# A graph network's fourth layer: the sums over edges one quad further behind their products

## The chip, the cores and the metric

The kernel runs on one core of a Trainium2 chip. The core has five engines that work side by side and wait for one another through semaphores: TensorE (PE in the profile; its weight loads are PEld), VectorE (DVE), ScalarE (ACT), GpSimd (POOL) and SyncE (SP). The metric is the device time of one execution in microseconds (us), the median of several runs.

## The reference

Four graph layers run one after the other on 8192 nodes and 262144 edges, which are sorted by their destination. Each layer adds a message sum to the node features (32 per node) and normalises. The change concerns the last one, layer 3, cut here to what it computes:

```python
h = relu(edge_feat @ W1 + b1)                      # E x 64
w = (h @ W2 + b2).reshape(e, 4, 8, 8)              # E x 256: four 8x8 matrices an edge
w_000, w_011, w_101, w_110 = w[:, 0], w[:, 1], w[:, 2], w[:, 3]
s_e, v_e = s[src], v[src]                          # gathered node features: 8 scalars, 8 vectors of 3
m0 = ALPHA * (einsum('ei,eio->eo', s_e * sh0, w_000) + C110 * einsum('eim,em,eio->eo', v_e, sh1, w_110))
m1 = ALPHA * (einsum('ei,em,eio->eom', s_e, sh1, w_011) + einsum('eim,eio->eom', v_e * sh0, w_101))
out0 = segment_sum(m0, dst) + SI_SCALE * (s @ si_w0)
out1 = segment_sum(m1, dst) + SI_SCALE * einsum('nim,io->nom', v, si_w1)
x = layernorm(x + concatenate([out0, out1]))
```

## The kernel before

Layers 0 to 2 come first and are done at about 4640 us of the profile. Layer 3 is the code from L748 (`cut = Carve()`) to the end of `raw_layers`. All its buffers are cut by hand out of one arena of SBUF, so the profile calls all of them `f_arena`; all PSUM is `bank`, eight banks of 512 words.

The edges stand in tiles of 128 (one edge a partition). Four tiles make a *quad* (512 edges), two quads a *group* (1024 edges), and eight quads a block of 32 tiles. There are NQ = 512 quads. One loop runs over the turns q; in each turn instructions are issued to all engines, and each engine carries out its own in that order. Waits are written out by hand: `mark` gives an instruction's number on its engine's semaphore, `after` waits for such numbers, and an engine skips a wait that it has already had.

What a turn q issues:

- **TensorE, hidden products** (`hidden`, L875, matmuls at L882), in even turns, for quads q+2 and q+3. ScalarE takes them from bank 2 through a ReLU into the buffers `hs` (L890).
- **TensorE, W2 products of quad q** (L906): four matmuls of 65 x 128 by 65 x 256, into one of two pairs of banks that take turns (`w_bank`). They wait for `hs` and for `w_free`, the end of VectorE's turn q-2, which read the same pair of banks.
- **GpSimd, gathers for quad q+12** (`fetch_rows`, L383): four indirect DMAs of 128 node rows each, released by the W2 products of quad q.
- **TensorE, sums over edges of quad c = q-3** (L915): four matmuls of a one-hot matrix `oh` (128 edges by 128 destinations) with the products `p` (128 edges by 344 columns), added up in bank 0 or 1 over the two quads of a group. They wait for VectorE's turn c+2 (`quad[c + 2]["v"]`), because the last 24 columns of `p` of quad c are written two turns after its other columns.
- **VectorE, a turn**: every eighth turn, the preparation of the next block (`factors`, L824 to L835), which waits for that block's gathers; the last 24 columns of `p` of quad q-2 (L930); a reduction for quad q-1 (L935); then, after the W2 products of q, five multiplications from PSUM into `p` and `pr` (L943, L946, three of L950) and the one-hot matrix of q (L505). The end of L505 is the mark `v` of the turn. Ahead of writing, a turn waits for the sums that last used its buffers, `quad[q - NP]["a"]`.
- **VectorE, a group's sums**: in every second turn, after its mark `v`, it reduces the bank of the group that ends with quad q-3 into `win` (L972, L973, L975), and sets the bank free (`agg_free`). Eight times in the layer the shifted windows are then summed on TensorE (`windows`, L495) and 1024 nodes are normalised (`normalize`, L454 to L464).

The buffers `p` and `oh` each have five copies (NP, NO). What the change touches is the number of those copies, the distance of 3 between W2 products and sums, and the turn in which VectorE takes up a group.

Of the kernel before, what the change touches and what calls it, by code (L numbers as in the profile page):

```python
# [105 lines left out]
def in_order(ctx: ExitStack, tc, x, a, w0, w1, b1, w2, si, keep):  # L106
# [34 lines left out]
    with tc.tile_critical():  # L141
        raw_layers(tc, x, a, w0, w1, b1, w2, si, m, bad)
# [3 lines left out]
def raw_layers(tc, x, a, w0, w1, b1, w2, si, m, bad):  # L146
# [438 lines left out]
    NO = 4  # L585
# [16 lines left out]
    def fetch_rows(g, h, let):  # L602

        if g < GG:
            G.after(let)
            gathers(ytab, row, g * GT // WT, g * GT % WT + h * GT // 2, GT // 2)
            if h == 1:
                landed[g] = under_way[-1]
# [30 lines left out]
    for g in range(GG + 2):  # L639
# [8 lines left out]
        h, bk, c = g % NO, (g // per) % 2, g % per  # L648
# [69 lines left out]
    for n, (l, c) in enumerate(seq):  # L718
# [8 lines left out]
        for s in range(64):  # L727
            if l == 1:
                q = s % 4
# [35 lines left out]
    a1 = cut(WT, 8)  # L765
    vm = cut(2, WT, 3, 8)
    MW = 344
    NP, NO = 5, 5
    p = cut(NP, 4, MW)
    pr = cut(2, 4, 64)  # L770
    red = cut(2, 4, 8)
# [22 lines left out]
    NQ = TT // 4  # L794
# [80 lines left out]
    def hidden(q):  # L875

        s = q // 8
        k = s % 3
        PE.after(batch[s]["e"], quad.get(q - 1, {}).get("h", h_free))
        for h in range(2):  # L880
            r = q % 4 + h
            ins = PE.e.matmul(bank[64 * h:64 * h + 64, 2, :], w1_s[r * D:(r + 1) * D, :],  # L882
                              ef[r * D:(r + 1) * D, k, (q % 8) // 4, :], start=True, stop=True,
                              tile_position=(r * D, 64 * h))
        pm = PE.mark(ins)
        if q % 8 == 6:
            ef_free[k] = pm
        for h in range(2):
            A.after(pm, quad.get(q + h - 4, {}).get("w"))
            quad[q + h] = dict(h=A.mark(A.e.activation(hs[0:64, (q + h) % 4], bank[64 * h:64 * h + 64, 2, :], AF.Relu,  # L890
                                                       bias=b1_s[64 * h:64 * h + 64])))
# [3 lines left out]
    factors(0)  # L895
    PE.after(c_in)
    hidden(0)
    for q in range(NQ + 4):

        if q % 2 == 0 and q + 2 < NQ:  # L900
            hidden(q + 2)
        if q < NQ:
# [4 lines left out]
            quad[q]["w"] = PE.mark(ins)  # L907
            quad[q]["k"] = k, wp
            fetch_rows(q + AHEAD)
        c = q - 3  # L910
        if 0 <= c < NQ:
            g = c // 2
            PE.after(quad[c + 2]["v"], agg_free[g % 2] if c % 2 == 0 else None)
# [14 lines left out]
        if 0 <= q - 2 < NQ:  # L928
            c = q - 2
# [35 lines left out]
                if s + 3 < NS:  # L965
                    fetch(s + 3)

        c = q - 3
        if 0 <= c < NQ and c % 2 == 1:
            g = c // 2  # L970
            V.after(quad[c]["a"])
# [483 lines left out]
```

## Time and profile before

| | |
|---|---|
| median of 3 runs | 7594.48 us (7588.88 to 7602.49) |
| the profiled execution | 7684.33 us, span 7682.3 us |
| PE busy | 5356.7 us (70% of the span) |
| DVE busy | 4365.5 us (57%) |
| POOL busy | 3983.9 us (52%) |
| ACT busy | 1629.8 us (21%) |
| layer 3: first W2 product, last sum over edges | 4637.5 us, 7660.9 us |
| layer 3: first and last gather issued | 4564.2 us, 7599.5 us |

All times inside the execution are microseconds from the start of the span. A row of the groups by line names line, engine, operation, what it writes and reads, shapes and count; then the busy time and the mean of one in ns; then the idle time of the engine just before these instructions, with who ended it. Each matmul of this layer is in fp32 and shows as two records, so the four of a quad are "x8". The recorded ends of matmuls are modelled. A row of the waits has the waiting engine and line, whom it waited for, the time in total, the number of waits and the longest. Shares of PEclk are tenths of TensorE's full clock, as granted in each fortieth of the span.

### The profile page before, as it was taken

To read this page: it belongs to the slowest core of one execution; us is meant where nothing else is said; L and a number is where in the kernel's file an instruction comes from. 1 tells how busy PE (TensorE), PEld (TensorE's weight loads), DVE (VectorE), ACT (ScalarE), POOL (GpSimd) and SP (SyncE) were. 2 spreads that over 40 slices of the span, in tenths; PEclk is the share of its full clock that TensorE was granted. 3 is DMA by queue.
4 is the path that set the end of the run, shared out by engine and by line. 5 is a ranking of instruction groups with operands and counts; after the bars stand their busy time and mean duration, and the time that the engine had idled before them with its cause. 6 is when DMAs were issued, how large, how long until landed. Compare 5 with 4: busy or idle time off the path is not lost.

```text
span 7682.3 us, 85779 instructions
## 1 busy us (share of the span) xinstructions
PE 5356.7 (70%) x34036; PEld 3776.5 (49%) x34036; DVE 4365.5 (57%) x8312; ACT 1629.8 (21%) x2812; POOL 3983.9 (52%) x4174
## 2 busy tenths in 40 slices
PE   5326565666666665665445768888888888888888
PEld 2115555555555555554222435555555555555555
DVE  3336666666666766765000005667666666666666
ACT  3213333333333333332000001111111111111111
POOL 3466565656565566651000016666666666666663
PEclk6556666666666667667777878999998999898999
DMA  8415554555455454557999961111111111111111
GB/s 279 149 41 145 135 148 138 145 138 148 138 143 149 135 149 134 148 137 268 433 431 429 401 265 20 24 24 24 23 24 24 24 24 24 24 24 23 24 24 19
DMA packets 290731, 999.29 MB, mean 130 GB/s; under 512 B 99021, under 2 KB 175886, under 8 KB 250638
## 3 DMA queue, kind: packets, MB, share of 16 engines
q1 hardware_dynamic: 155742, 916.89, 30.6%
q0 software_dynamic: 134144, 73.67, 10.4%
q8 instruction: 269, 4.41, 0.2%
q10 hardware_dynamic: 432, 3.15, 0.1%
q14 instruction: 144, 1.18, 0.1%
HBM read 521.39 MB, written 471.99 MB: 129 GB/s over the span
## 4 chain that ended last, share of the span: by engine, by line
PE 53%; DVE 12%; another core or an unknown queue 11%; DMA 10%; issue 8%; ACT 6%; POOL 0%; SPq 0%; DVEq 0%; ACTq 0%; POOLq 0%
PE bank L571 18%; PE bank L915 17%; PE bank L906 9%; DMA f_arena<-famat 6%; PE bank L882 3%; ACT f_arena L576 3%; DMA f_arena<-fcmat 3%; DVE f_arena L950 2%; ACT f_arena L575 2%; PE bank L730 2%; DVE f_arena L505 2%; PE bank L733 2%; DVE f_arena L946 1%; PE bank L657 1%
## 5 line engine op out<-in xcount | busy, mean ns | idle before, releaser
L383 POOL DMA_INDIRECT f_arena<-fxtab,f_src x2048 | 1959.1, 957 | 2146.6 <-DVE f_arena L786 1069.3
L383 POOL DMA_INDIRECT f_arena<-fytab,f_row x2048 | 1957.6, 956 | 1344.5 <-issue 548.4
L571 PE MATMUL bank<-f_arena 64*128 64x128 f32 x16384 | 1623.1, 374 | 959.3 <-issue 550.8
L571 PEld LDWEIGHTS bank<-f_arena 64*128 64x128 f32 x16384 | 1507.0, 279 | 1076.1 <-issue 899.3
L915 PE MATMUL bank<-f_arena 128*128 128x344 f32 x4096 | 1477.2, 508 | 320.3 <-DVE f_arena L505 307.2
L915 PEld LDWEIGHTS bank<-f_arena 128*128 128x128 f32 x4096 | 847.4, 211 | 790.4 <-DVE f_arena L505 364.0
L575 ACT ACTIVATE f_arena<-bank 128x512 bf16<-128x512 f32 x1024 | 613.0, 599 | 1973.2 <-PE bank L571 949.7
L906 PE MATMUL bank<-f_arena 65*128 65x256 f32 x4096 | 1011.3, 390 | 0.0
L906 PEld LDWEIGHTS bank<-f_arena 65*128 65x128 f32 x4096 | 769.5, 193 | 359.8 <-issue 226.7
L890 ACT ACTIVATE f_arena<-bank,f_arena 64x512 f32<-64x512 f32 x512 | 351.1, 686 | 2566.1 <-PE bank L882 955.0
L557 DVE TENSOR_TENSOR f_arena<-bank,f_arena 128x1024 f32<-128x1024 f32 x256 | 313.2, 1223 | 808.2 <-PE bank L571 323.9
L505 DVE TENSOR_TENSOR f_arena<-bank,f_rel 128x512 f32<-128x512 f32 (+1 forms) x768 | 659.0, 858 | 140.3 <-ACT f_arena L537 128.1
L576 ACT ACTIVATE f_arena<-bank 128x512 f32<-128x512 f32 x1024 | 611.5, 597 | 0.0
L559 DVE TENSOR_TENSOR f_arena<-bank,f_arena 128x2048 f32<-128x2048 f32 x256 | 586.6, 2291 | 8.8
L943 DVE TENSOR_TENSOR f_arena<-bank,f_arena 128x256 f32<-128x256 f32 x512 | 215.5, 421 | 651.0 <-PE bank L906 352.4
L950 DVE TENSOR_TENSOR f_arena<-bank,f_arena 128x256 f32<-128x256 f32 x1536 | 550.7, 414 | 0.0
L730 PE MATMUL bank<-f_arena,f_x_b 128*32 128x256 f32 x4096 | 295.0, 459 | 334.4 <-DMA f_arena<-famat 334.4
L657 PE MATMUL bank<-f_arena 128*128 128x96 bf16 x2048 | 252.0, 253 | 320.7 <-issue 173.8
L730 PEld LDWEIGHTS bank<-f_arena,f_x_b 128*32 128x32 f32 x4096 | 145.9, 132 | 472.5 <-DMA f_arena<-famat 309.5
L946 DVE TENSOR_TENSOR f_arena<-bank,f_arena 128x512 f32<-128x512 f32 x512 | 348.7, 681 | 0.0
L454 DVE TENSOR_TENSOR f_lnf<-bank,f_x_b 128x256 f32<-128x256 f32 x8 | 3.4, 424 | 606.4 <-PE bank L710 606.4
L657 PEld LDWEIGHTS bank<-f_arena 128*128 128x128 bf16 x2048 | 144.1, 118 | 413.3 <-issue 277.0
(133 smaller groups left out, 3539.5 us busy)
## 6 DMA issues: line engine op xcount, KB each, us to landing
famat<-f_arena SPq DMA_DIRECT2D x256, 1024.0 KB
fcmat<-f_arena SPq DMA_DIRECT2D x256, 512.0 KB
fytab<-f_arena SPq DMA_DIRECT2D x64, 1024.0 KB
f_arena<-fytab,f_row POOLq DMA_INDIRECT x2048
f_arena<-fxtab,f_src POOLq DMA_INDIRECT x2048
f_arena<-laid_ea SPq DMA_DIRECT2D x64, 512.0 KB
f_arena<-laid_ea SPq DMA_DIRECT2D x64, 64.0 KB
f_arena<-laid_xT ACTq DMA_DIRECT2D x1, 1024.0 KB, 8.3
```

Of the source, the lines that this page charges most:

```text
L383: return G.e.indirect_dma_start(out=dest, out_offset=None, in_=table, in_offset=bass.IndirectOffsetOnAxis(ap=ix, axis=0))
L505: return V.e.tensor_tensor(o, iota[:, None, :].to_broadcast([P, n, P]), rel[:, t:t + n, None].to_broadcast([P, n, P]), op=OP.is_equal)
L559: V.e.tensor_tensor(oh_l[:, b], iota[:, None, :].to_broadcast([P, 16, P]), meta_l[:, pp, k0:k0 + 16, None].to_broadcast([P, 16, P]), op=OP ...
L571: ins = PE.e.matmul(bank[:, bk + h, :].rearrange("p (c s j) -> p c s j", s=64, j=4)[:, :, :, j], oh_l[hs_, b, 4 * q + j, :], oh_k[hs_, b, ...
L575: A.e.activation(st_c[:, b, q], bank[:, bk:bk + 2, 0:256], AF.Copy)
L576: bank_free[units[0] % 2] = am = A.mark(A.e.activation(st_a[:, b, q], bank[:, bk:bk + 2, 256:512], AF.Copy))
L657: ins = PE.e.matmul(bank[:, bk, 3 * c * D:3 * (c + 1) * D], oh[:, h, t, :], xp[:, g % 4, t].rearrange("p c f -> p (c f)"), start=(t == 0), ...
L730: ins = PE.e.matmul(bank[q * D:(q + 1) * D, b, 0:256].rearrange("p (u h j) -> p u h j", h=2, j=4), x_b[:, s, :], mv[:, s], start=(s < 4), ...
L906: ins = PE.e.matmul(wp[:, t, :], hs[0:65, q % 4, t * P:(t + 1) * P], w2_s[0:65], start=True, stop=True)
L915: ins = PE.e.matmul(bank[:, g % 2, 0:MW], oh[:, c % NO, t, :], p[:, c % NP, t, :], start=(c % 2 == 0 and t == 0), stop=(c % 2 == 1 and t = ...
L946: V.e.tensor_tensor(pq[:, :, 0:128].rearrange("p t (o k) -> p t o k", k=16), wp[:, :, 0:128].rearrange("p t (o k) -> p t o k", k=16), a0[: ...
L950: V.e.tensor_tensor(pq[:, :, 128 + 64 * mm:192 + 64 * mm].rearrange("p t (o i) -> p t o i", i=8), wp[:, :, 192:256].rearrange("p t (o i) - ...
```

## The change

The sums over edges of quad c are issued in turn c+4 instead of c+3, behind the W2 products of quad c+4. VectorE takes up a group's sums in turn c+5, c being the group's last quad, instead of c+3; TensorE has issued that quad's sums one turn earlier, where before it issued them in the same turn. `p` and `oh` get a sixth copy each, and the loop runs for 518 turns instead of 516. What the sums wait for is written as before (`quad[c + 2]["v"]`), which is now VectorE's turn q-2 instead of q-1.

```diff
-    NP, NO = 5, 5
+    NP, NO = 6, 6
+    LAG3 = 4
...
-    for q in range(NQ + 4):
+    for q in range(NQ + LAG3 + 2):
...
-        c = q - 3
+        c = q - LAG3
         if 0 <= c < NQ:
             g = c // 2
             PE.after(quad[c + 2]["v"], agg_free[g % 2] if c % 2 == 0 else None)
...
-        c = q - 3
+        c = q - LAG3 - 1
         if 0 <= c < NQ and c % 2 == 1:
             g = c // 2
             V.after(quad[c]["a"])
```

## The prediction

> **What bounds the kernel now.** I first read the page's forty slices, to place layer 3.
>
> ```profile
> PE   5326565666666665665445768888888888888888
> DVE  3336666666666766765000005667666666666666
> POOL 3466565656565566651000016666666666666663
> PEclk6556666666666667667777878999998999898999
> ```
>
> From slice 25 on, PE is busy eight tenths, VectorE and GpSimd six: layer 3, from about 4640 us to the end. Nothing before it is changed. Next, the groups of instructions by line between 4640 and 7660 us, and TensorE's waits there.
>
> ```profile
> L383 POOL DMA_INDIRECT f_arena<-fxtab,f_src x2000 | 1913.8, 957 | 1062.9 <-issue 542.9 <-PE bank L906 268.4 <-PE bank L915 131.3
> L915 PE MATMUL bank<-f_arena 128*128 128x344 f32 x4093 | 1476.3, 508 | 320.3 <-DVE f_arena L505 307.2 <-issue 12.8
> L906 PE MATMUL bank<-f_arena 65*128 65x256 f32 x4092 | 1009.4, 389 | 0.0
> L943 DVE TENSOR_TENSOR f_arena<-bank,f_arena 128x256 f32<-128x256 f32 x512 | 215.5, 421 | 651.0 <-PE bank L906 352.4 <-PE bank L915 139.6 <-remote 83.3
> ...
> PE bank L915 <- DVE f_arena L505: 307.2, 138, 4.0
> ```
>
> TensorE waits almost only at L915 (sums over edges), for L505, the last VectorE instruction of a turn: 138 times, 307 us. VectorE waits 651 us for the W2 products, so the two wait for each other in a ring. GpSimd's waits other than its own issue end with TensorE. The last matmul of L915 starts at 7660.9 us and the first W2 product at 4637.5 us: 3023 us for 512 quads, 5.90 us each. The chain of waits between 6002 and 6020 us shows one stop of the ring.
>
> ```profile
> 6002.48 1.73 PE bank L906 x8
> 6004.21 2.32 PE bank L915 x8
> 6006.53 1.22 PE bank L882 x4
> ...
> 6009.79 0.61 DVE f_arena L505
> 6010.40 0.04 issue
> 6010.44 4.27 PE bank L915 x8
> ```
>
> Unhindered, a quad's W2 products take 1.73 us, its sums 2.32 us. After a stop the same eight records take 4.27 us, so a stop costs its idle time and 1.95 us more. Last, the timeline between 6018 and 6029 us (start, duration, idle before and who ended it):
>
> ```profile
> 6018.69 1.07 PE L882 MATMUL bank<-f_arena 32*64 32x512 f32 x4
> 6019.70 1.99 PE L906 MATMUL bank<-f_arena 65*128 65x256 f32 x8
> 6021.53 2.48 PE L915 MATMUL bank<-f_arena 128*128 128x344 f32 x8
> 6023.85 1.89 PE L906 MATMUL bank<-f_arena 65*128 65x256 f32 x8
> 6025.17 1.40 ACT L890 ACTIVATE f_arena<-bank,f_arena 64x512 f32<-64x512 f32 x2 [15.85 <-PE bank L915]
> 6025.26 0.42 DVE L943 TENSOR_TENSOR f_arena<-bank,f_arena 128x256 f32<-128x256 f32 x1 [5.54 <-PE bank L915]
> 6026.74 0.94 POOL L383 DMA_INDIRECT f_arena<-fxtab,f_src  x1 [0.30 <-issue]
> 6027.93 1.52 PE L915 MATMUL bank<-f_arena 128*128 128x344 f32 x2 [2.18 <-DVE f_arena L505]
> ```
>
> The hidden products (L882) end at 6019.76 by the record, but their reader on ScalarE starts at 6025.17. The W2 products end at 6021.69, and VectorE starts on them at 6025.26, 3.6 us later. TensorE's completions thus reach the others late at times, here by up to 5.4 us. The previous L882 (6006.53 to 6007.75 in the chain) was answered at 6007.93, within 0.2 us. The profile does not tell me why; I carry the lateness as an unknown.
>
> **What the Trainium skill says.** "TensorE: Matmul & The Clock Gate", What's actually happening: the array runs at half clock after about 3.4 us of little activity, and needs about as long of work to get back. The trace agrees in kind (4.27 against 2.32 us), but here a stop of 1 to 2 us is enough at times. "Perfetto Trace Analysis", Tensor Engine Instruction: a matmul's recorded end is estimated, and its semaphore comes when PSUM acknowledges the write. That allows the lateness; it doesn't give its 5.4 us. "DMA: Bandwidth & Descriptors", SWDGE vs HWDGE vs iDMA: GpSimd's cores write each descriptor of such a gather, so a gather occupies GpSimd. The trace agrees: 957 ns and 0.30 us to the next. "SBUF — State Buffer", SBUF: two separate sides: VectorE and GpSimd share a pair of ports, which one can hold against the other. The gathers' median is 945 ns against a minimum of 938, so hardly any of it shows here.
>
> **The change, part by part.**
>
> 1. The sums' wait. In turn q TensorE issues W2 of q, then the sums of q-3, which wait for VectorE's turn q-1. Afterwards they are the sums of q-4 and wait for turn q-2. W2 of q has already waited for that turn, since there are two W2 banks. So this wait is removed, and the first wait for turn q-1 is W2 of q+1, one set of sums later (2.32 us, with L882 3.3 to 3.5 us). In the stretch 6010.44 to 6027.93 us (three sets of sums, 17.49 us) the stop of 2.18 us is then covered by 2.32 us of sums, and the slow restart (1.95 us) goes: 13.4 us, 4.5 us a quad.
>
> 2. The new place of the wait. Ring: turn q-1 ends, W2 of q+1 (1.73), lateness L, VectorE's products L943 to L505 (6007.78 to 6010.40, 2.6 us): 4.4 us + L for two quads. TensorE's own two quads take 2 x (1.73 + 2.32) + 1.1 = 9.2 us. The ring is covered up to L = 4.8 us. At 5.4 us it costs 0.6 us, a short stop.
>
> 3. VectorE takes up a group's sums at q-5. TensorE did those in turn q-1, before W2 of q, whose completion VectorE has had. So the waits of L972 (about 240 us over the layer in all) go. They stand on VectorE, ahead of the next turn, and end with the ring; I don't count them twice. The bank is freed one turn later (L975): the sums of even q-4 need turn q-2's group sum, 0.8 us after that turn's end, behind the 1.73 us of W2. No wait while W2 takes longer than 0.8 us; without that cover, 0.8 us in every second turn (205 us).
>
> 4. Six buffers of p and oh for five: a buffer is reused in turn q after the sums of q-6, done in TensorE's turn q-2, as were those of q-5 before. No instruction is added; the cost is memory (1888 words a partition).
>
> 5. One more set of sums (2.3 us) behind the last products: +2.5 us once. The eight places where normalisation enters the ring stay. The gathers are still issued by GpSimd after W2 of q for quad q+12, the edge loads still by SyncE: both now earlier, as the turns are shorter. Nothing passes anything in their queues.
>
> What is late next: TensorE's floor is 512 x 4.6 = 2355 us, plus about 100 us at the eight normalisations (an estimate: some 10 us of stop and 4 us of L495 each), so 2455. GpSimd issues a gather every 957 + 300 ns, in undisturbed rows 1.25 us, so 5.0 us a quad. It starts 12 quads ahead, has 2000 to go from 4641 us, and so ends at 4641 + 2500 = 7141 us instead of 7599.5: no more than 458 us can go. The two floors are close, and VectorE's preparation of each eight quads (about 4 us) needs the last gather of them. For late completions, short stops and restarts I leave 60 us, an estimate (0.6 us of every fifth quad). Gain 458 - 60 = 398 us, 5.1 us a quad.
>
> The profiled execution took 7684.3 us for a span of 7682.3; with 398 less it would take 7286. The median is 7594.5, or 0.988 of it. I scale the gain: 393, so **7200 us**.
>
> **Rivals.**
>
> *A, as above*: TensorE runs on, and GpSimd's gathers become the bound. For: rows of 2.32 and 1.73 us whenever nothing is waited for, and GpSimd at 1.25 us. 7200 us, own range 7130 to 7300. Chance 0.62.
>
> *B, late completions keep half of it.* With L near 6 us in most turns the ring is 10.4 us for two quads, and stops with restarts bring it to about 5.5 us a quad: 0.4 x 512 = 205 us gained, 7390 us (7300 to 7480). For: more work without a pause could mean later completions. Against: the chain also shows prompt ones. 0.21.
>
> *C, GpSimd is quicker than its profile* (the 0.30 us between gathers partly the profiler's): TensorE's floor, 2455 for 3023 us, leaves 7040 to 7110 us. 0.05.
>
> *D, it does nothing*: the wait moves to W2 whole, which needs stops longer than 2.3 to 3.5 us throughout. Their mean is 307 / 138 = 2.2 us. 7590 us, 0.03.
>
> *E, slower.* Completions become later still because TensorE no longer pauses. The ring exceeds today's 11.8 us for two quads from L = 7.4 us on; at 8.2 us it is 12.6, 6.3 us a quad, +205 us: 7800 us. For: after the stops shown, completions are prompt, and a pause may be what lets them catch up. Against: 5.4 us is the longest in the stretch shown, and it came after TensorE had run for 15 us. 0.09.
>
> **How the numbers follow.** A measurement of this kernel can tell about 0.2% (15 us) from no change. Faster: A, B and C, 0.88. Same: D, 0.03. Slower: E, 0.09. The range 7110 to 7440 leaves out E, D, most of C and the upper part of B, about 0.2.
>
> **What would show it.** Step 1: L915's idle time falls from 320 us to below 60 us, and its mean from 508 ns towards 460 ns. Step 2: TensorE's waits for L505 stand at L906. Step 3: L972 has no idle time left. The bound: GpSimd's idle time goes down to its own issue (about 0.30 us each), the last gather starts near 7150 to 7200 us, and VectorE waits for gathers at the preparation. Wrong if L906 takes over more than 150 us of waits, if ScalarE's answers to L882 come later than 6 us as a rule (B, E), or if a gather takes clearly more than 957 ns.

## The result and the profile after

The kernel after takes 7578.29 us (median of 9 runs, 7571.73 to 7589.08), the kernel before in the same set of runs 7602.49 us (9 runs, 7588.46 to 7607.30). The ratio is 0.9973, with a 95% interval of 0.9963 to 0.9984: 24 us faster by the medians, where 393 us were forecast. The profiled execution of after took 7583.78 us for a span of 7581.8.

I measure layer 3 in all kernels as the time from the start of the first W2 product to the end of the last sum over edges, divided by 512 quads. It was 5.906 us a quad before (4637.5 to 7661.3 us) and is 5.793 after (4595.0 to 7561.0 us), 58 us less. Layer 3 also starts 42 us earlier, though nothing ahead of it was changed. The profiled execution of before was also 90 us above its median. Two single executions therefore differ by more than the change, and the 58 us are not its worth; the 24 us of the medians are.

One fact is needed to read the numbers below: later sets of runs executed the same kernel before in 6476 to 6489 us instead of 7602 to 7639, so I call this set and that of e1 to e4 the *first sets*, those of e5 to e16 the *later sets*, and compare only inside a set. In the code after, lines behind the loop's start have moved by one: hidden products L883, ScalarE L891, W2 products L907, sums L916, VectorE's products L944, a group's sums L973.

The forty slices of the page, after:

```profile
PE   5326665556555665654544867889989988888998
...
PEclk7557677777777777777777877999998999899989
```

TensorE has gone from eight tenths to between eight and nine. Next, the groups by line between 4640 and 7660 us; the columns are those of the tables above.

```profile
L383 POOL DMA_INDIRECT f_arena<-fxtab,f_src x1970 | 1892.8, 961 | 967.4 <-issue 541.5 <-remote 177.4 <-PE bank L907 175.8
L916 PE MATMUL bank<-f_arena 128*128 128x344 f32 x4056 | 1406.7, 489 | 65.4 <-issue 63.7
L907 PE MATMUL bank<-f_arena 65*128 65x256 f32 x4020 | 1048.4, 403 | 176.2 <-issue 161.0 <-DVE f_arena L505 14.2
...
L944 DVE TENSOR_TENSOR f_arena<-bank,f_arena 128x256 f32<-128x256 f32 x504 | 211.3, 419 | 829.7 <-remote 320.1 <-PE bank L907 318.7 <-PE bank L916 129.0
L973 DVE TENSOR_REDUCE f_arena<-bank 128x8 f32<-128x128 f32 x255 | 71.3, 280 | 6.7 <-PE bank L916 6.7
```

The 307.2 us in which the sums waited for L505 are gone. Only 14.2 us of waits for L505 stand at the W2 products. But TensorE now has 161.0 us at L907 and 63.7 us at L916 that end with "issue": it waited for no semaphore that the profile shows. VectorE waits longer for TensorE than before (829.7 against 651.0 us), and GpSimd still waits for it as well. All of them wait for TensorE, and TensorE hardly waits for them: 14.2 us here, and 53.7 us at the eight normalisations (L495).

The timeline of after, from 6003 us on (start, duration, then the idle time before):

```profile
6002.83 1.07 PE L883 MATMUL bank<-f_arena 32*64 32x512 f32 x4
...
6003.84 1.99 PE L907 MATMUL bank<-f_arena 65*128 65x256 f32 x8
...
6008.94 1.56 PE L907 MATMUL bank<-f_arena 65*128 65x256 f32 x6 [0.79 <-issue]
...
6011.84 0.59 PE L907 MATMUL bank<-f_arena 65*128 65x256 f32 x1 [1.34 <-issue]
...
6013.24 0.59 PE L907 MATMUL bank<-f_arena 65*128 65x256 f32 x1 [0.81 <-issue]
...
6014.64 1.88 PE L916 MATMUL bank<-f_arena 128*128 128x344 f32 x3 [0.81 <-issue]
...
6014.74 1.40 ACT L891 ACTIVATE f_arena<-bank,f_arena 64x512 f32<-64x512 f32 x2 [19.00 <-PE bank L907]
6014.83 0.43 DVE L944 TENSOR_TENSOR f_arena<-bank,f_arena 128x256 f32<-128x256 f32 x1 [5.32 <-PE bank L907]
```

The hidden products end at 6003.90 by the record; ScalarE, which had been idle for 19 us, gets them at 6014.74, 10.8 us later. The W2 products recorded up to 6005.83 are answered at 6014.83. Just ahead of these answers TensorE's records crawl: one matmul at 6011.84, one at 6013.24. Over the layer, the time from a hidden product's recorded end to ScalarE's start has a median of 0.82 us, a third quartile of 5.0 and a maximum of 10.9; before they were 0.09, 2.5 and 7.2. So either only the news of TensorE's completions came late, or its recorded starts and ends ran ahead of what it had done, by up to 10.9 us and further than before. e1 decides between the two.

### The profile page after: what moved, and what is told of

The parts are those of the page before. It is cut to its first block, busy times and chain, and to the rows that moved or that the text cites. A ratio compares the mean times of both kernels' runs of the same rounds, so it can differ in the third digit from the quotient of the medians.

```text
span 7581.8 us, 85791 instructions
## 1 busy us (share of the span) xinstructions
PE 5254.6 (69%) x34036; PEld 3717.5 (49%) x34036; DVE 4352.7 (57%) x8312; ACT 1629.6 (21%) x2812; POOL 3996.6 (53%) x4174
## 4 chain that ended last, share of the span: by engine, by line
PE 55%; another core or an unknown queue 11%; DMA 11%; issue 9%; DVE 8%; ACT 5%; POOL 0%; SPq 0%; DVEq 0%; ACTq 0%; POOLq 0%
PE bank L571 18%; PE bank L916 14%; PE bank L907 11%; DMA f_arena<-famat 7%; PE bank L657 3%; PE bank L883 3%; DMA f_arena<-fcmat 3%; ACT f_arena L576 3%; PE bank L730 2%; PE bank L733 2%; ACT f_arena L575 2%; DVE f_arena L951 1%; DVE f_arena L505 1%; PE bank L495 1%
## 5 line engine op out<-in xcount | busy, mean ns | idle before, releaser
L571 PE MATMUL bank<-f_arena 64*128 64x128 f32 x16384 | 1566.7, 365 | 963.4 <-ACT f_arena L576 682.8
L571 PEld LDWEIGHTS bank<-f_arena 64*128 64x128 f32 x16384 | 1463.3, 272 | 1100.6 <-issue 938.7
L916 PE MATMUL bank<-f_arena 128*128 128x344 f32 x4096 | 1420.3, 489 | 65.4 <-issue 63.7
L907 PE MATMUL bank<-f_arena 65*128 65x256 f32 x4096 | 1075.3, 405 | 176.2 <-issue 161.0
L916 PEld LDWEIGHTS bank<-f_arena 128*128 128x128 f32 x4096 | 842.8, 207 | 509.3 <-issue 217.5
L907 PEld LDWEIGHTS bank<-f_arena 65*128 65x128 f32 x4096 | 785.2, 198 | 559.3 <-issue 361.0
L891 ACT ACTIVATE f_arena<-bank,f_arena 64x512 f32<-64x512 f32 x512 | 351.3, 686 | 2500.1 <-remote 1001.6
L505 DVE TENSOR_TENSOR f_arena<-bank,f_rel 128x512 f32<-128x512 f32 (+1 forms) x768 | 660.9, 861 | 139.9 <-ACT f_arena L537 127.7
L944 DVE TENSOR_TENSOR f_arena<-bank,f_arena 128x256 f32<-128x256 f32 x512 | 214.7, 419 | 845.0 <-PE bank L907 324.4
L730 PE MATMUL bank<-f_arena,f_x_b 128*32 128x256 f32 x4096 | 293.2, 457 | 344.9 <-DMA f_arena<-famat 344.9
L657 PE MATMUL bank<-f_arena 128*128 128x96 bf16 x2048 | 216.7, 222 | 357.7 <-issue 215.5
L730 PEld LDWEIGHTS bank<-f_arena,f_x_b 128*32 128x32 f32 x4096 | 145.1, 131 | 481.8 <-DMA f_arena<-famat 318.0
L657 PEld LDWEIGHTS bank<-f_arena 128*128 128x128 bf16 x2048 | 122.0, 104 | 404.5 <-issue 260.2
```

The costliest lines, as they stand in the source:

```text
L505: return V.e.tensor_tensor(o, iota[:, None, :].to_broadcast([P, n, P]), rel[:, t:t + n, None].to_broadcast([P, n, P]), op=OP.is_equal)
L571: ins = PE.e.matmul(bank[:, bk + h, :].rearrange("p (c s j) -> p c s j", s=64, j=4)[:, :, :, j], oh_l[hs_, b, 4 * q + j, :], oh_k[hs_, b, ...
L657: ins = PE.e.matmul(bank[:, bk, 3 * c * D:3 * (c + 1) * D], oh[:, h, t, :], xp[:, g % 4, t].rearrange("p c f -> p (c f)"), start=(t == 0), ...
L730: ins = PE.e.matmul(bank[q * D:(q + 1) * D, b, 0:256].rearrange("p (u h j) -> p u h j", h=2, j=4), x_b[:, s, :], mv[:, s], start=(s < 4), ...
L907: ins = PE.e.matmul(wp[:, t, :], hs[0:65, q % 4, t * P:(t + 1) * P], w2_s[0:65], start=True, stop=True)
L916: ins = PE.e.matmul(bank[:, g % 2, 0:MW], oh[:, c % NO, t, :], p[:, c % NP, t, :], start=(c % 2 == 0 and t == 0), stop=(c % 2 == 1 and t = ...
```

## The experiments

My theory after the result: in the first sets TensorE stops by itself (without waiting for another engine), and its waits for VectorE were where that time showed, not its cause. The first rival: the ring between TensorE and VectorE still binds, only through later completions (the prediction's B and E). The second: GpSimd's gathers bind (A).

### e1: TensorE without the ring

The kernel after with VectorE's turns left out: the preparation, the products and the one-hot matrices are not computed, `p` and `oh` hold constants, and the sums add those up. Hidden, W2 products, sums, a group's sums, gathers and loads stay.

```diff
+    V.e.memset(p, 0.01)
+    V.e.memset(oh, 0.01)
...
-            PE.after(quad[c + 2]["v"], agg_free[g % 2] if c % 2 == 0 else None)
+            PE.after(agg_free[g % 2] if c % 2 == 0 else None)
...
-            V.e.tensor_tensor(pr[:, q % 2]...
...
-            ins = one_hot(oh[:, q % NO], 4 * q, 4)
```

> VectorE's turns of layer 3 are left out (no products, no one-hot matrices; p and oh hold a constant), so that TensorE waits for no turn; hidden products, W2 products, sums, groups and gathers stay. Lateness only (TensorE could go on at its recorded speed and it is only the news of its completions that is late): a quad takes 4.6 to 4.8 us, the layer about 2450 us, some 550 us less than after. TensorE itself is the limit (the records run ahead of the real work): a quad takes 5.6 to 5.9 us as in the changed kernel, with crawling matmuls in it.

Measured: 7572.17 us (one run; before in this set 7638.93, 31 runs). Layer 3 takes 5.743 us a quad (4609.3 to 7549.8 us), though TensorE waits for no turn of VectorE; the only wait for another engine that its profile shows in the layer is 5.7 us for ScalarE. Were only the news late, the layer would have gone down to about 2450 us. The busy time in five successive stretches of its profile (window and its length; busy time and count of PE, PEld, DVE, ACT, POOL; then granted clock, DMA share, GB/s):

```profile
6004.70:6007.40 2.70, 1.46 (x5) 0.44 (x4) 0.00 (x0) 0.00 (x0) 0.18 (x1) 1.00 0.05 6
6007.50:6014.20 6.70, 6.70 (x14) 4.51 (x14) 0.97 (x4) 1.37 (x2) 4.71 (x5) 0.50 0.36 103
6014.40:6028.60 14.20, 14.20 (x56) 9.56 (x54) 0.74 (x3) 1.37 (x2) 10.38 (x11) 1.00 0.08 13
6028.70:6031.30 2.60, 1.63 (x5) 0.51 (x4) 0.00 (x0) 0.00 (x0) 0.07 (x1) 1.00 0.02 2
6031.40:6038.10 6.70, 6.70 (x15) 4.58 (x15) 0.74 (x3) 1.37 (x2) 5.18 (x6) 0.50 0.07 12
```

A period of 24.0 us: 2.6 us in which five matmuls are recorded and VectorE and ScalarE get no answer, then 6.8 us at half clock, then 14 us at full clock. Between two stops lie 144 records of TensorE, 72 matmuls and 72 weight loads, which is four quads. A stop costs its 2.7 us and half of the 6.8 us at half clock, 6.1 us of 24.0; the rest is 17.9 us for four quads, 4.5 us each, as its last eight quads take (4.50 us), which come behind the last gather. The sum closes for the whole layer too, as an estimate: the clock is at half for 562 us of it, which costs 281 us, and 128 stops (one in four quads) of 2.65 us cost 339 us; without both, 4.53 us a quad are left of the 5.743. So the ring is not the bound here. With all waits for VectorE's turns gone, and VectorE's work with them, the kernel is 67 us faster than before in its set (7572.17 against 7638.93 us): about as much as a new arrangement of these waits could gain.

### e2: where the stop is

The kernel after, with the sums of q-4 waiting for the W2 products of q. TensorE can then not run ahead in the records.

```diff
         if 0 <= c < NQ:
             g = c // 2
+            PE.after(quad.get(q, {}).get("w"))
```

> The changed kernel, and TensorE waits for the completion of its own W2 products of quad q before the sums of q-4. Lateness comes of streaming without a pause: with the pause ScalarE and VectorE start within 0.2 us of the recorded end, the ring is covered and the layer falls to 5.0 to 5.2 us a quad, 7200 to 7300 us in all. Lateness has another cause (gathers, memory): TensorE waits as long as VectorE does today, nothing is gained, and the stops make it slower, 7700 to 8000 us.

Measured, with before at 7638.93 us: 7752.75 us (4 runs), ratio 1.0146 (1.0115 to 1.0177), 6.106 us a quad. The timeline shows TensorE waiting for itself:

```profile
6039.44 1.89 PE L907 MATMUL bank<-f_arena 65*128 65x256 f32 x8
6044.14 0.43 DVE L945 TENSOR_TENSOR f_arena<-bank,f_arena 128x256 f32<-128x256 f32 x1 [3.23 <-remote]
6044.16 3.25 PE L917 MATMUL bank<-f_arena 128*128 128x344 f32 x6 [2.83 <-remote]
```

The W2 products end at 6041.33; VectorE and TensorE both go on at 6044.14 to 6044.16. Most other W2 products (303 of 376) are answered within 0.06 us, and then one comes late: TensorE waits more than 1 us 132 times, 312 us together, with a median of 2.8 us. Between two late ones there are mostly (99 of 131 times) again 144 records, which take about 24.5 us and hold 16 gathers. I read the 10.9 us of after, therefore, as a stop of 2.8 us plus records that had run ahead. This run can't tell 16 gathers from 144 records.

### e3 and e4: one half of the change each

e3 issues the sums four quads behind, with six buffers, and takes up a group in the turn of its sums. e4 keeps the distance of 3 and takes up a group one turn later, also with six buffers.

```diff
 e3, against after
-        c = q - LAG3 - 1
+        c = q - LAG3
 e4, against after
-        c = q - LAG3
+        c = q - 3
...
-        c = q - LAG3 - 1
+        c = q - 4
```

> The sums four quads behind, but VectorE takes a group up in the turn that issues its last sums, as before. If the longer distance is what changes the time: 7560 to 7600 us, within 0.2% of the changed kernel, with waits of L973 back at some 100 to 250 us that end with the ring. If the later taking up is what counts: near 7600 us, as the kernel before.

> The sums three quads behind as before, but VectorE takes a group up one turn later; six buffers. If the longer distance is what changes the time: 7590 to 7610 us, the kernel before. If VectorE's wait for the group's sums was part of the ring: 7560 to 7590 us, as the changed kernel.

Measured, with before at 7638.93 us: e3 7627.02 us, ratio 0.9987 (0.9981 to 0.9994), 5.836 us a quad. e4 7655.37 us, ratio 1.0023 (1.0013 to 1.0032), 5.904 us a quad. The longer distance gains something alone; taking up the group later, alone, loses a little, which neither of its forecasts had. In e3 VectorE waits 289 us at L973, and still gains; in e4 it waits 5.0 us at L972, and doesn't. Why e4 loses I did not find out.

### e5 to e7: gathers or records, in a later set

e5 is e2 with the gathers from quad 32 on left out (old rows are used instead). e6 is e2 with four more W2 products of one column a quad, which adds records without gathers. e7 is a bare stream on TensorE: besides what e1 leaves out, the hidden products, ScalarE's part and the edge loads are left out, and `hs` is constant.

```diff
 e5, beside e2's line
-            rows[q // 8] = gathers(xtab, src, q // 8, q % 8 * 4, 4)
+            if q < 32:
+                rows[q // 8] = gathers(xtab, src, q // 8, q % 8 * 4, 4)
+            else:
+                rows[q // 8] = rows[q // 8 - 4]
...
 e6, beside e2's line
+                PE.e.matmul(wp[:, t, 0:1], hs[0:65, q % 4, t * P:(t + 1) * P], w2_s[0:65, 0:1], start=True, stop=True)
+            for t in range(4):
...
 e7, beside e1's edit
...
-            quad[q + h] = dict(h=A.mark(A.e.activation(hs[0:64, (q + h) % 4], bank[64 * h:64 * h + 64, 2, :], AF.Relu,
-                                                       bias=b1_s[64 * h:64 * h + 64])))
+            quad[q + h] = dict(h=hm)
```

> As the run with TensorE's wait for its own W2 products, and GpSimd gathers only the first 32 quads' rows (the later quads use those rows again, so the result is of other edges). In that run the W2 products' completion came about 2.8 us late in every fourth quad and promptly otherwise. Gathers or their memory traffic hold TensorE up: those late completions go, 5.1 to 5.4 us a quad. TensorE stops by itself: they stay, 2.8 us in every fourth quad, about 6.1 us a quad, total within 1% of that run.

> As the run with TensorE's wait for its own W2 products, with four more matmuls of one column a quad ahead of them (16 more records, 52 for 36; their results are written over). Stops come by the number of TensorE's instructions (one in about 145): a stop in every 2.8 quads, and with the added work of about 0.8 us some 7.2 to 7.6 us a quad. Stops come by time (about every 24.5 us) or by quads: still one in 24 us or in four quads, 6.9 to 7.0 us a quad.

> TensorE alone as before, and without hidden products and ScalarE: only W2 products and sums (4.05 us a quad by their rows, 32 records), waiting for nobody but the group's sums. Stops by the number of instructions: one in 4.5 quads, 4.7 us a quad, and up to 5.3 with slow stretches of the clock. TensorE can't take the matmuls at their recorded pace at all: 5.0 to 5.2 us a quad without single long stops. No limit of its own: 4.1 us a quad.

Measured, with before at 6485.05 us: e5 6497.44 us and 5.110 us a quad, e6 7271.65 us and 6.617, e7 6406.25 us and 4.112. In this set TensorE didn't stop: in e5 every answer to its hidden products came within 0.12 us and, after the first 65 us of the layer, its clock was at half for only 6.8 us, and e7 ran nearly at the rate of the records (1.73 + 2.32 = 4.05 us). But before was 15% faster here too, so e5 and e6 say nothing on the trigger, although 5.110 us lies in the range that was to mean "gathers", and e6 is quicker than both its forecasts. They show that the stops belong to the set, and what TensorE can do without them. e1 to e7 ran on a chip of one and the same number, so another chip doesn't explain the difference.

### e8 to e10: both kernels in a later set

e8 is the kernel before, e9 the kernel after, e10 is e2 again.

> The kernel before once more, for its trace beside those of this set. If TensorE stops by itself in this set too (the kernel before at about 7600 us): completions up to 5.4 us late, 5.9 us a quad. If it doesn't (as in the set before this one, 6485 us): completions within 0.3 us, few stops at the sums, 5.0 to 5.1 us a quad, bound by the gathers (1.25 us each).

> The changed kernel once more. Where TensorE stops by itself (before at about 7600 us): 0.997 of the kernel before, as measured. Where it doesn't (before at 6485 us): the waits that the change removes are short there, and the gathers bound both, so 0.985 to 1.0 of the kernel before; 5.0 us a quad.

> The changed kernel with TensorE's wait for its own W2 products. Where TensorE stops by itself: 1.015 of the kernel before, as measured. Where it doesn't: completions are prompt anyway and the wait costs some 0.3 to 0.5 us a quad of TensorE's time, which the gathers hide: 1.00 to 1.03 of the kernel before.

Measured, with before at 6476.40 us (17 runs): e9 6476.05 us, ratio 1.0001 (0.9993 to 1.0010); e10 6502.03 us, ratio 1.0042 (1.0027 to 1.0058). Layer 3 takes 5.103 us a quad in e8, 5.092 in e9, 5.137 in e10. Groups by line of e8, between 3870 and 6420 us:

```profile
L383 POOL DMA_INDIRECT f_arena<-fxtab,f_src x2002 | 1912.0, 955 | 620.1 <-issue 517.8 <-DMA f_arena<-fxtab,f_src 55.8 <-PE bank L906 20.6
L915 PE MATMUL bank<-f_arena 128*128 128x344 f32 x4011 | 1304.9, 468 | 112.0 <-DVE f_arena L505 112.0
```

And of e9, in the same window:

```profile
L383 POOL DMA_INDIRECT f_arena<-fxtab,f_src x2003 | 1906.4, 952 | 622.5 <-issue 531.2 <-DMA f_arena<-fxtab,f_src 49.7 <-PE bank L907 24.3
L916 PE MATMUL bank<-f_arena 128*128 128x344 f32 x4019 | 1283.1, 461 | 0.0
L907 PE MATMUL bank<-f_arena 65*128 65x256 f32 x4024 | 997.3, 391 | 64.6 <-DVE f_arena L505 64.6
...
L829 DVE TENSOR_TENSOR f_arena<-f_arena 128x768 f32<-128x768 f32 x63 | 60.6, 962 | 214.8 <-DMA f_arena<-fxtab,f_src 213.0
...
L495 PE MATMUL bank<-f_arena,f_shift 128*128 128x256 f32 (+1 forms) x98 | 39.5, 588 | 52.0 <-DVE f_arena L976 52.0
```

Here the prediction's picture stands: no idle time at L916, its mean at 461 ns, GpSimd with hardly more than its own issue (1906.4 + 622.5 = 2529 us for 2003 gathers, 1.26 us each), VectorE waiting for gathers at the preparation (64.1 us at L828 in e8, 213.0 here). The gathers bind. They bind in e8 as well, so the change gains nothing. The 112.0 us of TensorE's waits at the sums come back in other places: 64.6 us at L907, and 52.0 us at L495, where e8 has 7.5. VectorE is late there because its gathers are.

### e11 to e16: the change without gathers, and repeats

e11 is the kernel before and e12 the kernel after with e5's cut of the gathers, without e2's line. e13 repeats e6 and e14 repeats e7; in another set e15 repeats e12 and e16 repeats e6.

> The kernel before, with gathers for the first 32 quads alone (later quads use those rows again). Where TensorE doesn't stop by itself and the gathers bind: 4.7 to 4.9 us a quad instead of 5.1, the ring of sums and turns showing. Where TensorE stops by itself: 5.8 to 5.9 us as with gathers, if the gathers aren't the cause; below 5.2 if they are.

> The changed kernel with the same cut. Where TensorE doesn't stop by itself: 4.6 to 4.7 us a quad, 0.1 to 0.2 us below the kernel before with that cut, which is what the change is worth when nothing else binds. Where TensorE stops by itself: 5.7 to 5.8 us if the gathers aren't the cause, below 5.0 if they are.

> TensorE's wait for its W2 products and 16 more records a quad, once more. Where TensorE doesn't stop by itself: 6.6 us a quad, as in the first run. Where it does: a late completion in every 2.8 quads and 7.2 us or more a quad if stops come by the number of instructions; one in four quads, or in about 24 us, if not.

> The bare stream of W2 products and sums, once more. Where TensorE doesn't stop by itself: 4.1 us a quad, as in the first run. Where it does: 4.7 us or more, with a stop in every 4.5 quads if they come by the number of instructions.

> The changed kernel with gathers for the first 32 quads alone. Without stops in this set: 4.8 us a quad as before. With stops: 5.7 to 5.8 us if the gathers aren't their cause, below 5.0 if they are.

> TensorE's wait for its W2 products and 16 more records a quad. Without stops in this set: 6.6 us a quad as before. With stops: 7.2 us or more and a late completion in every 2.8 quads if they come by the number of instructions, one in four quads or 24 us if not.

Measured, with before at 6479.78 us: e11 6395.54 us (4.918 us a quad), e12 6332.70 us (4.799), e13 7263.23 us, e14 6396.89 us; with before at 6489.34 us: e15 6328.88 us (4.799 again), e16 7262.06 us. No stops in these sets either, so the trigger stays untested. What e11 and e12 do show is the worth of the change when neither the gathers nor TensorE's stops bind: 63 us, 1.0% (one run each). Both layers are slower than their forecasts (4.7 to 4.9 and 4.6 to 4.7), the gap between them is as forecast. The sums' group in e11, between 3870 and 6300 us:

```profile
L918 PE MATMUL bank<-f_arena 128*128 128x344 f32 x3958 | 1253.7, 458 | 56.1 <-DVE f_arena L505 56.1
```

and in e12:

```profile
L919 PE MATMUL bank<-f_arena 128*128 128x344 f32 x4060 | 1264.6, 453 | 0.0
```

The wait that part 1 names is gone, and its 56.1 us are most of the 63.

### What the traces say of the trigger

Since no kernel without gathers ran in a first set, I looked for stretches without gathers inside the first sets. In after the last gather is issued at 7499.07 us, and the W2 products of ten quads start behind it. Busy time by stretch, ahead of that, and behind it (columns as in e1):

```profile
7453.00:7499.00 46.00, 41.51 (x148) 26.97 (x147) 31.65 (x82) 4.58 (x7) 31.00 (x33) 0.93 0.09 13
...
7508.00:7561.00 53.00, 52.81 (x201) 35.74 (x200) 42.37 (x114) 4.71 (x7) 0.00 (x0) 1.00 0.00 1
```

With gathers, TensorE is busy for 41.5 of 46 us, at a mean clock of 0.93. Without them it is busy for 52.8 of 53 us at full clock, its last eight quads at 4.53 us each, and every hidden product is answered within 0.05 us. The other five profiles of the first sets show the same: from 4 us behind the last gather on, no answer to a hidden product is late. The edge loads had ended by 7445.6 us, and stops still came between 7453 and 7505 us, so it is not those. Loads of instructions don't fit either: e1 has 33 of them in 1000 us (24 and 9 on the two queues), and a stop about every 24 us. The stretch of L730 in the middle of the kernel has no gathers either: in before its 48 answers on ScalarE come within 0.15 us of the last recorded matmul, and it takes 617.6 us there and 617.5 us in e8, though it loads far more, while the stretch of L571, which gathers, takes 3056 us in the one and 2423 us in the other. So stops appear where gathers are under way, and not in the two stretches without any. That is where they appear, not why: gathers go on in the later sets as well, without stops, and no run of a first set took them away.

What counts off 144 records I could not settle. In the L571 stretch of after, 208 of 244 intervals between answers that are over 3 us late also have 144 records, but last about 12 us instead of 24 and mostly hold 8 gathers instead of 16. That speaks against time and against the number of gathers. But 144 records are also whole turns of the loops of both stretches. Nor do I know why some sets have stops and others none.

## Why the prediction was wrong

The sign was right in this set, by 0.3%, and the size was not: 24 us for 393. In a later set even the sign is gone (e9: ratio 1.0001).

**Part 1 (the sums' wait), right in mechanism.** L505 ends none of the sums' idle time: 307.2 us to nothing, idle 320.3 to 65.4 us (forecast: below 60). The mean fell only from 508 to 489 ns instead of towards 460, since the slow restarts stayed: they follow TensorE's own stops. In e9, without stops, it is 461 ns.

**Part 2 (the new place of the wait), right where it says the wait is covered.** 14.2 us stand at L907. The lateness L did grow past 4.8 us, up to 10.9, as rivals B and E feared, though not "as a rule": 41 of 256 answers to hidden products came later than 6 us, 10 before. But their price was wrong: I charged L to the ring as a delay for TensorE. It was TensorE's stop itself, seen by the others (e1: with no ring at all 5.743 us a quad). So E's loss didn't come.

**Part 3 (the group), right as a reading, worth little.** The idle time at the group's first sum is 6.7 us, from about 240. VectorE had the time to spare: e4, which takes up groups later and changes no distance, is 0.2% slower.

**Parts 4 and 5 (buffers, tail).** No run tests them alone; e4 has the sixth buffers too and gains nothing.

**The step that failed: "TensorE's floor is 512 x 4.6 = 2355 us, plus about 100 us".** I took 1.73 and 2.32 us from records of undisturbed rows and held them for a rate that TensorE can keep. In the first sets it can't: e1's layer took 2940 us, 485 us more than my 2455. Of the 458 us of room, TensorE itself leaves about 67 (e1 against before in its set), and the medians show 24 taken. The 60 us "for late completions, short stops and restarts" were this term: in e1 stops and half clock come to some 620 us (281 + 339, the estimate there). Why TensorE stops stays open. From it followed the second fault, that GpSimd becomes the bound: the last gather is issued at 7499.07 us, not at 7150 to 7200, and its idle time still ends with TensorE. Without stops the floor was sound: e12's layer, without gathers either, took 2457 us, though with less time at the normalisations than the sum has.

**What the prediction had in hand.** It showed the lateness (5.4 us) and left it "as an unknown" inside the ring. "Perfetto Trace Analysis", Tensor Engine Instruction, in the Trainium skill, says that a matmul's recorded end is an estimate; after shows 10.8 us between one such end and its answer, and starts that run ahead with it. The row spacings rest on the same records, so they alone were no floor. The last eight quads of before, at 4.62 us and with prompt answers, could have been set beside the 5.90 us of the layer. And "TensorE waits for L505" was a loop read from one side: in the stretch that the prediction shows, VectorE was late because TensorE's W2 products came late.

**GpSimd's floor was right, for another set.** 5.0 us a quad were forecast for the gathers, 5.1 for the layer; e9 shows 5.092. But before reaches 5.103 there (e8), so the number came true without the gain that was to bring it.

No version that computes the whole result beat both kernels.

## What to carry to other kernels

A floor for TensorE is not the spacing of its records in a good stretch: it is what TensorE takes when it waits for no other engine, so measure it by feeding it constants (e1, e7), or compare the layer's end, where other work has stopped, with its middle. When the engine that others wait for shows a wait of its own, ask whether its partner was late because of it; here completions that were answered up to 10.9 us late meant that it was behind, while its busy share had gone up. And a gain at one wait is bounded by the next engine's own pace: here about 67 us of room in one set, nothing in another, and 63 us only once the gathers were taken away.

## What the hardware showed that I had not expected

- TensorE stopped without a wait that the profile shows, for 2.6 to 2.9 us about every 144 of its records (24.0 us in e1, 24.5 us in e2), mostly with half clock around the restart: 6.8 us of it in the stretch of e1, 3.4 us at 95 of the 132 late answers of e2, none at 19. The stops were seen only where gathers were under way, and only in some sets of runs.
- "TensorE: Matmul & The Clock Gate", What's actually happening, in the Trainium skill, gives about 3.4 us of little activity ahead of half clock; here 2.6 us of it were enough (e1), and in e8, which has no stops, even a wait of 1.29 us at 4343 us: the sums behind it took 4.28 us, at half clock for 3.4 of them.
- The recorded starts of matmuls, not only their ends, ran ahead of the work, by up to 10.9 us in after; with one semaphore wait a quad on TensorE (e2) three quarters of the answers to hidden products came within 0.05 us.
- Between the first and the four later sets the stretches of the kernel before that gather differ, and the stretch of L730 does not. What differs between the sets I don't know.
- Four more products of one column a quad cost 1.48 us a quad (6.617 us in e13 against 5.137 in e10, in different sets). About 0.67 us of it is half clock: e13's clock is at half for 748 us of its layer, e10's for 64, although TensorE is busy by its records for 3351 of e13's 3388 us.
